# The output projection of the first pass as seven products too, and the sums of its weights made in that pass

## The chip, the cores and the metric

The kernel runs on one core of a Trainium2 chip. The metric is the time of one execution on the device, in microseconds (us). All data is float32.

## The reference, cut to what matters

Two transformer blocks work on 2048 tokens of width 512 (8 sequences of 256 tokens). The change lies in the attention of the first block, a linear attention with 32 heads of 128, whose result is projected back to width 512:

```
qkv  = silu(xn @ qkv_w.T)                  # 32 heads, q, k and v of 128 each
attn = (decay * (q @ k.T)) @ v             # per head and sequence, in causal form
gate = sigmoid(xn @ gate_w.T)
out  = (gate * norm_w * rms(attn)) @ out_w.T       # [tokens, 4096] @ [4096, 512]
```

A mixture of 16 experts (two for each token) and a shared expert are added to the same result; the second block (one more attention and 64 low-rank experts) comes last. The last product, with `out_w`, is the one that the change rewrites in a quarter of the tokens.

## The kernel before, in words

**Passes, units and products.** The attention runs in four passes (`i` from 0 to 3) over 512 tokens each, that is two sequences (`b`). A pass has eight units (`g`), each with four heads in two pairs. A unit computes q, k, v and gate for its heads in seven "outer" products, p1, p2, p6, p5, p3, p7, p4 (`ORDER`; `k` counts them from 0 to 6): it is a Strassen-like scheme in which seven products of sums of blocks stand for eight products of blocks. In passes 1 to 3 each outer product is again made of seven inner ones; in pass 0 the three of `RAW` (p1, p2, p4) are made of seven, and the other four in plain form (`Outer.plain`, eight inner products). One inner product is `product` (line 731), four matmuls into one PSUM bank.

**Weights in the first pass.** `weights` (lines 662 to 703) loads each outer product's weights from `in_w_att` into one of three ring buffers `w` (line 679), and blocks to be added into two staging buffers `st` (line 674). VectorE makes the outer sums; GpSimd makes four inner sums (`inner_sum`, line 692), and the last of them has the sums stored to DRAM in `ws` (line 694), from which the later passes load them ready made. A ring buffer is free for the load three outer products later when that store has landed. These steps are issued one per inner product, during the outer product before theirs. For the products of `RAW` the matmuls use GpSimd's inner sums already in the first pass.

**The output product.** When an outer product has completed a pair of heads for one sequence, a `Quarter` begins: activations, scores (lines 853 and 854), the product with v (865 and 866), a square for the norm (880, whose sum is made on GpSimd) and the gated result `gT`, [128, 2, 256] (885). `Unit.output` then queues the output product. In plain form (`project_plain`) each quarter gives two pieces of four matmuls, eight pieces in a unit. In the form of seven products (`project`, line 942) there are seven such pieces in a unit; four sums of `gT` are needed as operands. The weights of p1, p2 and p3 are quarters of `in_w_out` as they are; those of p4, p5, p6 and p7 are sums of quarters (p5's tile holds the fourth quarter until its sum is made in place). Before the change pass 0 is plain, pass 1 has seven products and makes the four sums of weights on GpSimd (`out_sum`, line 1002) and stores them in `wos` (line 1003), and passes 2 and 3 load them from there (line 987). The last unit of pass 3 is plain in both kernels.

**Accumulation.** Each piece is added on VectorE into `acc`, seven blocks of [128, 512] per pass (ScalarE copies the first ones). In the form of seven products the blocks are not yet the result: `combine` makes it out of them at the end of a pass with seven additions on GpSimd, and `finish` (line 642) follows.

**Order.** Pieces of a quarter, output products, sums of weights and the like are put on a list with a due time (`later`) and released by `slot()`, which runs once after each inner product, so that a unit has 49 slots; most pieces count, and a slot gives out one of them (two if more than 12 wait). ScalarE and GpSimd keep the order of the program. The order on TensorE, VectorE and SyncE, which issues nearly all DMAs, is made by a planner from the program's order and its own costs. Each engine, and SyncE's queue too, then works strictly in that order: an instruction that waits holds up what is behind it.

**Buffers.** There are seven tiles for output weights (`wo`, 256 KB each), five for `gT`, and three PSUM banks (`ps_sc`) for scores and output products.

The functions that the diff touches, and their callers:

Of the kernel before, what the change touches and what calls it, by code (L numbers as in the profile page):

```python
# [22 lines left out]
NCH = NT // CH  # L23
# [4 lines left out]
NG = H // HG  # L28
# [41 lines left out]
def block_kernel(  # L70
# [25 lines left out]
    nc = tc.nc  # L96
    mm = nc.tensor.matmul

    def tt(o, a, b, op, eng=None):
        (eng or nc.vector).tensor_tensor(o, a, b, op)  # L100
# [32 lines left out]
    def ps_sc():  # L133
        return ps.tile([P, 512], FP, tag="sc", name="ps_sc", bufs=3)
# [101 lines left out]
    def rsqrt(o, v, scale=1.0):  # L236

        nc.scalar.activation(o, v, AF.Sqrt, bias=eps_t, scale=scale)
        nc.vector.reciprocal(o, o)

    class Normal:


        def __init__(self, o, xc):
            self.o, self.xc = o, xc
            self.mv = small.tile([P, TPC, 2], FP, tag="mv", name="mv")
            self.rstd = small.tile([P, TPC], FP, tag="rstd", name="rstd")
# [144 lines left out]
    def add(o, a, b, eng=None):  # L392
        tt(o, a, b, ALU.add, eng)

    def sub(o, a, b, eng=None):
        tt(o, a, b, ALU.subtract, eng)
# [259 lines left out]
    with tc.tile_pool(name="attn", bufs=1) as attn, tc.manual_schedule(engines={mybir.EngineType.Activation, mybir.EngineType.Pool}):  # L656
# [90 lines left out]
        def later(after, f):  # L747
            pieces.append((now[0] + after, len(pieces), f))
            pieces.sort(key=lambda x: x[:2])
# [144 lines left out]
        class Unit:  # L894
            def __init__(self, i, g):
                self.i, self.g = i, g
                self.tiles = {}
                self.wo, self.decays = {}, []
                self.A, self.O = {}, {}
                self.plain = i == 0 or (i, g) == (NCH - 1, NG - 1)  # L900

# [4 lines left out]
            def output(self, b, pair, gT):  # L908

                if self.plain:  # L910
                    for t in range(2):
                        later(4 + t, partial(self.project_plain, b, pair, gT, t))
                    return
                A, O = self.A, self.O
                pool = nc.gpsimd
                A[b, pair] = gT
                if (b, pair) == (0, 0):
                    O["p1"] = gT
                    ready = (("p1", 4),)
                elif (b, pair) == (1, 0):  # L920
                    O["p7"] = self.gated()
                    sub(O["p7"], A[0, 0], gT, pool)
                    ready = (("p7", 6),)
                elif (b, pair) == (1, 1):
                    O["p4"] = gT
                    O["p5"], O["p6"] = A[1, 0], A[0, 0]
                    add(A[1, 0], A[1, 0], gT, pool)
                    sub(A[0, 0], A[1, 0], A[0, 0], pool)
                    ready = (("p4", 4), ("p5", 7), ("p6", 10))
                else:  # L930
                    O["p2"] = gT
                    O["p3"] = A[1, 1]
                    sub(A[1, 1], gT, O["p6"], pool)
                    ready = (("p2", 4), ("p3", 7))
                for p, after in ready:
                    later(after, partial(self.project, p))
# [40 lines left out]
            def load_out(self, k):  # L977

                if self.plain:
                    for h in range(2):  # L980
                        if k in (2, 4):
                            self.out_tile((k // 2 - 1, h), w_out[self.g, k // 2 - 1, h])
                    return
                at = dict(p1=(0, 0), p5=(0, 1), p2=(1, 0), p3=(1, 1))
                for p in {2: ("p1",), 3: ("p7", "p4", "p5"), 4: ("p6", "p2"), 5: ("p3",)}.get(k, ()):
                    if p in ("p4", "p5", "p6", "p7") and self.i > 1:
                        self.out_tile(p, wos[self.g][:, int(p[1]) - 4].rearrange("p (h n) -> p h n", h=2))
                    else:
                        self.out_tile(p, w_out[self.g, at[p][0], at[p][1]] if p in at else None)
                if k == 5 and self.i == 1:  # L990
                    for n in range(4):
                        later(6 + 2 * n, partial(self.out_sum, n))

            def out_tile(self, key, source):
                self.wo[key] = attn.tile([P, 2, C // 2], FP, tag="wo", name="wo", bufs=7)
# [28 lines left out]
            def done(self):  # L1024
                if self.g < NG - 1:
                    return
                i = self.i
                pr = ps_sc()

                def squares(ts):  # L1030
                    for t in ts:
                        for n in range(2):
                            mm(
                                pr[:, t : t + 1],
                                sums_[i][:, t // 2, n * S + t % 2 * P : n * S + (t % 2 + 1) * P], ones,
                                start=(n == 0), stop=(n == 1),
                            )

                def means():
                    squares((2, 3))  # L1040
                    rms = small.tile([P, TPC], FP, tag="rms", name="rms", bufs=NCH)
                    rsqrt(rms, pr[:, 0:TPC], 1.0 / (H * HD))
                    all_rms[i] = rms

                def store():
                    nc.sync.dma_start(out=xs_[i], in_=self.r)

                squares((0, 1))
                later(1, means)
                after = 2  # L1050
                if 0 < i < NCH - 1:
                    for n in range(7):
                        later(after + n, partial(combine, i, COMBINED[n : n + 1]))
                    after += 8
                if i + 1 < NCH:
                    for n in range(TPC):
                        later(after + 1 + n, partial(finish, i, self.r, (n,), tc.keep_in_program_order))
                    later(after + 1 + TPC, store)
# [251 lines left out]
        for n, (i, g, p) in enumerate(plan):  # L1310
# [5 lines left out]
            k = ORDER.index(p)  # L1316
# [494 lines left out]
```

## Time and profile before

| what | value |
|---|---|
| median of 3 runs | 2814.0 us (2809.46 to 2821.68) |
| the profiled execution: its own time | 2814.99 us |
| its span, first to last instruction | 2813.1 us |
| pass 0, about | 130 to 735 us of the span |
| passes 1, 2, 3, about | 735 to 1330, 1330 to 1925, 1925 to 2515 us |
| one unit of pass 0, about | 72 to 75 us |
| TensorE matmul busy, share of the span | 98% |
| TensorE weight load busy, share of the span | 90% |
| VectorE, ScalarE, GpSimd busy | 58%, 34%, 59% |
| DMA moved | 752.66 MB, 268 GB/s on average |

The span is what the profile divides up; 1.9 us lie around it. PE is TensorE's matmul row and PEld its weight loads, DVE VectorE, ACT ScalarE, POOL GpSimd, SPq SyncE's queue of DMA issues. A matmul in float32 stands in the trace as two instructions, so that a piece of four matmuls is "x8". L100 is a helper through which most element-wise operations go; its operations are told apart by the names of their tiles. "A <- B" in a list of waits means that A stood idle until B was done.

### The profile page before, as it was taken

How to read it: one execution, taken by the hardware profiler on the slowest of the kernel's cores; microseconds unless marked ns; L12 is line 12 of the kernel's file. 1: busy time of each engine (PE TensorE's matmuls, PEld its weight loads, DVE VectorE, ACT ScalarE, POOL GpSimd, SP SyncE). 2: the span in 40 equal slices, each digit the busy share in tenths (PEclk: the TensorE clock that was granted, in tenths of full speed). 3: DMA queues.
4: the chain of work that ended last, by engine and by line, in shares of the span. 5: the costliest groups of instructions: out<-in, count | busy, mean ns of one | idle time of the engine just before them, and what ended most of it. 6: DMA issues, size and time to landing. Idle time of an engine off the chain costs nothing.

```text
span 2813.1 us, 49529 instructions
## 1 busy us (share of the span) xinstructions
PE 2752.4 (98%) x19653; PEld 2538.8 (90%) x19653; DVE 1630.7 (58%) x2722; ACT 947.6 (34%) x1683; POOL 1645.8 (59%) x1414
## 2 busy tenths in 40 slices
PE   9999999998999999999999999999999999999999
PEld 5699999998989999999999999999999999987877
DVE  7666777776445555555545555555455555656663
ACT  4232222221433333333343333333433333432211
POOL 6467777775566676666755555556555567642220
PEclk9999999999999999999999999999999999999999
DMA  7888888887977877778877777787777788662211
GB/s 276 322 339 337 319 330 329 322 317 293 346 273 288 290 288 273 288 277 299 316 264 261 261 271 261 264 311 279 282 271 265 270 312 305 221 222 77 68 55 62
DMA packets 155062, 752.66 MB, mean 268 GB/s; under 512 B 18721, under 2 KB 25249, under 8 KB 103457
## 3 DMA queue, kind: packets, MB, share of 16 engines
q1 hardware_dynamic: 136672, 678.67, 64.7%
q0 software_dynamic: 17872, 70.32, 7.6%
q8 instruction: 155, 2.54, 0.3%
q14 instruction: 75, 0.61, 0.1%
q10 hardware_dynamic: 288, 0.52, 0.1%
HBM read 605.66 MB, written 142.99 MB: 266 GB/s over the span
## 4 chain that ended last, share of the span: by engine, by line
PE 85%; DVE 6%; DMA 4%; issue 2%; POOL 2%; ACT 1%; another core or an unknown queue 0%; SPq 0%; DVEq 0%; POOLq 0%; ACTq 0%
PE ps_a L731 25%; PE ps_e L731 12%; PE ps_sc L942 10%; PE ps_b L731 7%; PE ps_o L865 4%; PE ps_sc L962 3%; PE ps_sc L853 3%; PE ps_sc L800 3%; PE ps_a L1601 2%; PE ps_o L866 2%; PE ps_sc L854 2%; PE ps_a L1701 2%; DMA st<-in_w_att_dram 2%; DVE w L100 1%; PE ps_sc L812 1%
## 5 line engine op out<-in xcount | busy, mean ns | idle before, releaser
L731 PE MATMUL ps_a<-xt,w 128*128 128x128 f32 x5376 | 752.9, 276 | 17.2 <-DVE r L100 7.8
L731 PEld LDWEIGHTS ps_a<-xt,w 128*128 128x128 f32 x5376 | 687.8, 192 | 47.3 <-issue 14.1
L100 POOL TENSOR_TENSOR c<-c 128x512 f32<-128x512 f32 x240 | 305.5, 1288 | 268.9 <-DVE c L100 266.5
L1099 ACT COPY cp<-ps_a 128x512 f32<-128x512 f32 x384 | 224.3, 584 | 667.7 <-PE ps_a L731 642.3
L100 POOL TENSOR_TENSOR c<-c,r 128x512 f32<-128x512 f32 x264 | 346.3, 1334 | 166.7 <-DVE r L100 164.2
L731 PE MATMUL ps_e<-xt,w 128*128 128x128 f32 x2688 | 374.8, 276 | 5.2 <-DVE c L100 1.6
L100 POOL TENSOR_TENSOR w<-w 128x512 f32<-128x512 f32 x224 | 298.2, 1339 | 93.2 <-DVE w L100 44.7
L731 PEld LDWEIGHTS ps_e<-xt,w 128*128 128x128 f32 x2688 | 341.3, 192 | 12.1 <-issue 4.8
L731 PE MATMUL ps_a<-w,xt 128*128 128x128 f32 x1792 | 346.9, 275 | 0.0
L100 POOL TENSOR_TENSOR sums<-sums,sq 128x512 f32<-128x512 f32 x120 | 155.9, 1299 | 280.9 <-ACT sq L880 280.4
L942 PE MATMUL ps_sc<-wo,gT 128*128 128x256 f32 x1288 | 304.9, 380 | 2.4 <-POOL gT L100 2.4
L731 PEld LDWEIGHTS ps_a<-w,xt 128*128 128x128 f32 x1792 | 272.6, 192 | 0.0
L942 PEld LDWEIGHTS ps_sc<-wo,gT 128*128 128x128 f32 x1288 | 232.9, 190 | 30.5 <-issue 2.9
L100 DVE TENSOR_TENSOR acc<-ps_sc,acc 128x512 f32<-128x512 f32 x208 | 142.6, 689 | 192.6 <-PE ps_sc L942 151.1
L885 DVE SCALAR_TENSOR_TENSOR gT<-ps_o,nw,c 128x256 f32<-128x256 f32 x256 | 111.9, 478 | 214.9 <-ACT sq L880 205.9
L731 PE MATMUL ps_b<-xt,w 128*128 128x128 f32 x1536 | 216.0, 277 | 13.1 <-DVE w L100 6.2
L100 DVE TENSOR_TENSOR c<-ps_a,c 128x512 f32<-128x512 f32 x216 | 146.8, 687 | 123.3 <-PE ps_a L731 118.5
L731 PEld LDWEIGHTS ps_b<-xt,w 128*128 128x128 f32 x1536 | 196.1, 194 | 16.0 <-issue 12.6
L828 ACT ACTIVATE c<-c 128x512 f32<-128x512 f32 x256 | 150.4, 628 | 145.8 <-DVE c L100 127.0
L880 ACT ACTIVATE sq<-ps_o 128x512 f32<-128x512 f32 x120 | 71.7, 597 | 367.0 <-PE ps_o L866 359.5
L100 DVE TENSOR_TENSOR s<-ps_sc,decay 128x384 f32<-128x384 f32 x256 | 139.5, 553 | 81.5 <-PE ps_sc L854 76.8
L731 PE MATMUL ps_e<-w,xt 128*128 128x128 f32 x896 | 173.5, 275 | 0.0
(306 smaller groups left out, 4747.4 us busy)
## 6 DMA issues: line engine op xcount, KB each, us to landing
w<-in_w_att_dram SPq DMA_DIRECT2D x128, 1024.0 KB
st<-in_w_att_dram SPq DMA_DIRECT2D x32, 1024.0 KB
wo<-in_w_out_dram SPq DMA_DIRECT2D x113, 256.0 KB
decay<-dec SPq DMA_DIRECT2D x64, 384.0 KB
w<-ws0p SPq DMA_DIRECT2D x12, 1792.0 KB
w<-ws1p SPq DMA_DIRECT2D x12, 1792.0 KB
w<-ws2p SPq DMA_DIRECT2D x12, 1792.0 KB
w<-ws3p SPq DMA_DIRECT2D x12, 1792.0 KB
```

Source lines behind the costliest of these rows:

```text
L100: (eng or nc.vector).tensor_tensor(o, a, b, op)
L731: mm(bank[:, bass.ts(ty, P)], a, b, start=(first and ty == 0), stop=True, skip_group_check=True,)
L800: mm(pu[:, bass.ts(n, P)], w12[:, n, c, :], self.xeT[:, c, :], start=(c == 0), stop=(c == NC - 1),)
L828: nc.scalar.activation(qk, qk, AF.Silu)
L853: mm(p[:, 0:S], self.c[:, 2 * hh, P : 2 * P], q, start=True, stop=True)
L854: mm(p[:, S : S + P], self.c[:, 2 * hh + 1, P : 2 * P], q[:, 1, :], start=True, stop=True,)
L865: mm(po[:, bass.ts(hh, S)], v[:, 0, :], self.s[:, hh, 0:S], start=True, stop=False)
L880: nc.scalar.activation(sq, po, AF.Square)
L885: nc.vector.scalar_tensor_tensor(gT[:, h, :].rearrange("p (t n) -> p t n", t=2), po[:, bass.ts(h, S)].rearrange("p (t n) -> p t n", t=2), ...
L942: mm(py[:, bass.ts(t, S)], self.O[p][:, hh, bass.ts(t, P)], self.wo[p][:, hh, :], start=(t == 0 and hh == 0), stop=(hh == 1), skip_group_c ...
L962: mm(py[:, bass.ts(h, S)], gT[:, hh, bass.ts(t, P)], self.wo[pair, h][:, hh, :], start=(h == 0 and hh == 0), stop=(hh == 1), skip_group_ch ...
L1099: nc.scalar.copy(c, bank)
```

## The change

Pass 0 makes its output product in the form of seven products too, and makes and stores the sums of weights there. Pass 1 then loads all its output weights, as passes 2 and 3 do. Two of the four sums of `gT` are made on VectorE in pass 0. In pass 0 the tiles of a unit's output weights are all taken at k = 3 (four loads from `in_w_out` and three empty tiles) instead of two at k = 2 and two at k = 4, and the four sums of weights are due 8, 10, 12 and 14 slots after that. `combine` now follows pass 0 too, so that `finish` of pass 0 comes eight slots later.

```diff
@@ class Unit
-                self.plain = i == 0 or (i, g) == (NCH - 1, NG - 1)
+                self.plain = (i, g) == (NCH - 1, NG - 1)
@@ def output
                 pool = nc.gpsimd
+                soon = pool if self.i else nc.vector
                 A[b, pair] = gT
...
                     O["p7"] = self.gated()
-                    sub(O["p7"], A[0, 0], gT, pool)
+                    sub(O["p7"], A[0, 0], gT, soon)
                     ready = (("p7", 6),)
...
                     O["p3"] = A[1, 1]
-                    sub(A[1, 1], gT, O["p6"], pool)
+                    sub(A[1, 1], gT, O["p6"], soon)
                     ready = (("p2", 4), ("p3", 7))
@@ def load_out
-                for p in {2: ("p1",), 3: ("p7", "p4", "p5"), 4: ("p6", "p2"), 5: ("p3",)}.get(k, ()):
-                    if p in ("p4", "p5", "p6", "p7") and self.i > 1:
+                order = {2: ("p1",), 3: ("p7", "p4", "p5"), 4: ("p6", "p2"), 5: ("p3",)}
+                if self.i == 0:
+                    order = {3: ("p1", "p3", "p5", "p7", "p2", "p6", "p4")}
+                for p in order.get(k, ()):
+                    if p in ("p4", "p5", "p6", "p7") and self.i > 0:
                         self.out_tile(p, wos[self.g][:, int(p[1]) - 4].rearrange("p (h n) -> p h n", h=2))
                     else:
                         self.out_tile(p, w_out[self.g, at[p][0], at[p][1]] if p in at else None)
-                if k == 5 and self.i == 1:
+                if k == 3 and self.i == 0:
                     for n in range(4):
-                        later(6 + 2 * n, partial(self.out_sum, n))
+                        later(8 + 2 * n, partial(self.out_sum, n))
@@ def done
-                if 0 < i < NCH - 1:
+                if i < NCH - 1:
                     for n in range(7):
                         later(after + n, partial(combine, i, COMBINED[n : n + 1]))
                     after += 8
```

## The prediction

> **What bounds the kernel now.** I read the page's table of engines first, then the stretches by pass, then who waits for whom on TensorE in the first pass, then one unit of it in order of time. The table, and the four passes (time; busy us of PE, PEld, DVE, ACT and POOL, with instruction counts; granted clock; DMA share; GB/s):
>
> ```profile
> PE 2752.4 (98%) x19653; PEld 2538.8 (90%) x19653; DVE 1630.7 (58%) x2722; ACT 947.6 (34%) x1683; POOL 1645.8 (59%) x1414
> ...
> 130.00:735.00 605.00, 584.80 (x4451) 561.16 (x4451) 409.94 (x607) 160.94 (x279) 423.37 (x359) 0.99 0.86 326
> 735.00:1330.00 595.00, 589.72 (x4509) 559.64 (x4508) 314.49 (x480) 223.74 (x404) 389.12 (x314) 1.00 0.78 285
> 1330.00:1925.00 595.00, 588.50 (x4492) 560.38 (x4491) 317.39 (x473) 226.48 (x404) 343.13 (x277) 1.00 0.76 279
> ```
>
> TensorE is the bound in every pass: its weight loads fill 93 to 94% of each. The first pass is the tightest for the others: TensorE stands idle 605.0 - 584.8 = 20.2 us, against 5.3 and 6.5 in the next two, POOL is busy 70%, DVE 68%, and DMA 86%. So work taken from TensorE there is worth its full length only while POOL, DVE and DMA still deliver in time. Who holds TensorE up in six of the units (the engine that waits and whom for; us, times, longest), and what does it once, at 667 us:
>
> ```profile
> PE ps_b L731 <- issue: 3.8, 2, 2.0
> PE ps_a L731 <- POOL w L100: 3.5, 5, 1.3
> PE ps_b L731 <- DVE w L100: 6.2, 1, 6.2
> ```
>
> The 3.5 us are small, but they fall at one place in five units, the inner sums of p4's weights. One such place in POOL's and SyncE's order (start, length, what, and the idle time ahead):
>
> ```profile
> 528.74 1.27 POOL L100 TENSOR_TENSOR sums<-sums,sq 128x512 f32<-128x512 f32 x1
> 532.49 1.27 POOL L100 TENSOR_TENSOR w<-w 128x512 f32<-128x512 f32 x1 [2.48 <-DVE w L100]
> ...
> 535.20 4.02 POOL L100 TENSOR_TENSOR w<-w 128x512 f32<-128x512 f32 x3
> 542.75 5.21 POOL L100 TENSOR_TENSOR w<-w 128x512 f32<-128x512 f32 x4 [3.53 <-issue]
> ...
> 522.88 6.25 SPq L694 DMA_DIRECT2D ws5p<-w  x2
> 529.19 1.54 SPq L997 DMA_DIRECT2D wo<-in_w_out_dram  x2
> 534.88 4.36 SPq L679 DMA_DIRECT2D w<-in_w_att_dram  x2
> ```
>
> POOL has gaps of 2.48 and 3.53 us. The second ends when p4's weights have landed: their load went out at 534.88, after SyncE had waited 4.1 us for the store of p5's sums (issued 522.88), and TensorE waits 0.38 us for the third of these sums at 546.66. p4's chain, store, load, sums, product, has no slack. p2's has 3.2 us: its first sum is done at 561.7, its second product comes at 564.86.
>
> **What the Trainium skill says.** "Perfetto Trace Analysis", section Identifying the Most-Contended Engine: matmul busy time is a poor measure, weight-load time a good one; hence the 93% above, which agrees. "GPSIMD Engine Reference", section Key points: it shares its SBUF interfaces with VectorE, with contention against VectorE instructions with two SBUF inputs. The trace agrees: such additions into w take VectorE 0.63 us at 671.85, where POOL is idle, and 1.16 at 676.58, where POOL works beside. "DMA: Bandwidth & Descriptors", section Issuing engines are not separate DMA queues: all DMAs share 16 engines; so 8 MB more in the first pass lengthen the landing of what is already there. Between 525 and 540 us this trace shows a DMA share of 1.00 at 392 GB/s. "TensorE: Matmul & The Clock Gate", section What's actually happening: after an idle window of some 3.4 us the array runs at half clock for about as long. After the stall at 667 us the granted clock was 0.55 and 0.77 in the next slices of 5 us.
>
> **Part by part.**
>
> 1. *TensorE.* Eight pieces a unit become seven. A piece takes 1.73 us from its start to the next instruction (510.27 to 512.00). 8 units x 1.73 = **-13.8 us**, all on the bound. The piece goes from k = 0 and 1 of each unit: pieces in k = 2 to 5, the stretch of p4's chain, stay four.
>
> 2. *VectorE, first pass.* 60 additions and 4 copies into acc become 49 and 7 (ScalarE: 3 x 0.59 us more, idle 70%). DVE loses 11 x 0.69 = 7.6 us and gains 16 sums of gT. No row of before has these on DVE: bounds 0.63 and 1.26 us (the w sums just named; the row of w<-w on DVE means 1.259), I take 1.26: +20.2. Net +12.6 us over the pass, 1.6 a unit beside some 22 idle: nothing, covered by DVE's idle time in k = 0, 1 and 6. In k = 2 and 3 DVE is full (510 to 525), and the sum for p3 and two more additions, 2.6 us, fall there; p5's sums there stand 2.4 us ahead of POOL's need, p3's 3 us ahead of TensorE's. If that cover is short, up to 0.5 us a unit.
>
> 3. *POOL, first pass.* 16 sums of gT x 1.275 (row of gT<-gT) = 20.4, and 32 sums of weights x 1.50 (row of wo<-wo) = 48.0: 8.5 us a unit, busy from 56 to about 65 of 73. The sums of gT fall at k = 1, where POOL stood idle 8.38 us before 503.29: nothing. The sums of weights fall due at k = 4 and 5, three of them ahead of p7's inner sums and one among them: 4 x 1.5 = 6.0 us into gaps of 2.48 + 3.53 = 6.01. p4's sums then start when they did. But p7's end 6.0 - 2.5 = 3.5 us later, so does their store, and p2's load waits for that store: 3.5 us against a slack of 3.2, less the 1.73 that TensorE is now early. Bounds 0 and 2.0 us a unit; I take 0.3, since the wait before p2's load is for the landing, and not all of the shift need arrive there.
>
> 4. *DMA and SyncE, first pass.* 32 stores of 256 KB = 8.4 MB more, 1.05 MB a unit. Output weights: as many loads, all at k = 3; 0.5 MB leave the full stretch at 529 and 0.5 MB leave 500, and 1 MB comes at 514, beside a trough (share 0.22 from 510 to 515). p3's tile is used until slot 23 of the next unit and its load is due at slot 21, so SyncE can stand some 3 us; p7's block and weights are queued behind, and p5's store behind those. SyncE waited there for p6's store until 522.46 anyway. For p4's chain: at best 0.5 MB less ahead of it, -1.2 us a unit (at 392 GB/s; only the present 0.4 to 1.3 can be gained); at worst 1.05 MB more, +2.7, and 0.8 of standing, +3.5. I take +0.1, since both signs are open. SyncE's waits for the sums before their stores (102 us for 32 in the second pass) move here; p1's load stands behind the last.
>
> 5. *Second pass.* 48 us of POOL work and its waits leave, 32 loads replace 32 stores. The third pass is of that form already, and TensorE idles 6.5 us in it against 5.3. Nothing; bounds -2 and +2. Its output loads wait for tiles 234 us in the third pass against 78 without TensorE standing, so that too is covered, by weights loaded a product ahead.
>
> 6. *Between the passes.* Seven combines x 1.3 = 9.1 us of POOL, finish eight slots later; a staging buffer is held as long, and the first copy into the next acc waits. The start of the third pass shows just that: ScalarE waits 9.2 us for finish, TensorE idles 1.2 and 1.7 us in two slices, no more than at the start of the second now (3.6 us). Nothing; bounds -1 and +3, a late expert's load the risk.
>
> Sum: -13.8 + 8 x (0.3 + 0.1) = -10.6, about **-11 us**. The profiled execution has 2815.0, the median 2814.0: so 2804 against the one, **2803** against the other.
>
> **Rivals.**
>
> *The stalls go too.* If early loads into the trough and fewer stores between p5's sums and p4's load give p4's chain slack, the 3.5 us of waits there go, and the one stall of 6.2 us at 667 with its slow clock after it (some 2 us), which comes from a staging block that landed late. For: the stretch 525 to 540 is full and loses loads. Against: it gains three stores. -13.8 - 3.5 - 6.2 - 2 = -25: **2789**.
>
> *p4's chain takes over (slower).* It has no slack, and TensorE's saving lies elsewhere, so each us by which p5's store or p4's load is late is a us of the unit. It decides from 1.73 us a unit, where the saving is gone; at 3.5 (item 4) the result is 8 x 3.5 - 13.8 = +14; with 1 us of half clock after each stall, +22: **2836**. For: DMA share 1.00 there, POOL's gaps filled to the last 0.1 us. Against: the trough at 510, and the planner, which may put stores behind the load.
>
> *The saving is eaten half.* Stalls of 0.8 to 1.7 us a unit, by the same places and p2's: -7 to 0, **2810**.
>
> That the change does not do what it says I see no way for: all eight units of the pass get the seven products.
>
> **How the numbers follow.** Forecast 0.50 (own range 2796 to 2808), stalls go too 0.17, half eaten 0.12, p4's chain 0.21. A measurement of this kernel can tell 0.5%, 14 us, from no change: 2800 and 2828. The forecast lies across the first border: its waits may be nil and the third item's 0.3 with it, and of its 0.50 I put 0.25 below 2800. Faster 0.25 + 0.17 = 0.42; same 0.25 + 0.12 = 0.37; slower 0.21. Range 2787 to 2832, from the first rival's value to most of the second's.
>
> **What would show it.** Right: 56 pieces at line 942 in the first pass and that pass 10 to 14 us shorter, the others as long; waits of p4's product for POOL at no more than 1.5 us a unit; sums of weights 1.5 us each inside POOL's two gaps; p4's load 12 us after p5's store as now. Wrong: waits of TensorE for POOL's or DVE's w above 14 us in the first pass; p5's store or p4's load later than now by over 1.7 us against the unit's start; a first pass as long as before; or a second pass that changes by over 3 us.

## The result, and the profile after

The kernel after takes **2857.75 us** (median of 4 runs, 2854.18 to 2860.86) against 2815.3 us for the kernel before beside it: a ratio of 1.015, 95% interval 1.0123 to 1.0177. The forecast was 2803 us, with a range that ended at 2832. The change makes the kernel 1.5% slower.

The profiled execution took 2854.18 us, with a span of 2852.5. The line of its page that answers to the first one of before:

```profile
PE 2753.9 (97%) x19589; PEld 2530.1 (89%) x19589; DVE 1643.0 (58%) x2727; ACT 947.5 (33%) x1686; POOL 1676.6 (59%) x1437
```

TensorE has less to do and is busy as long. The same stretches as before, cut at the new ends of the passes (time; busy us and counts of PE, PEld, DVE, ACT, POOL; granted clock; DMA share; GB/s):

```profile
130.00:774.00 644.00, 583.77 (x4373) 548.55 (x4373) 407.59 (x606) 162.56 (x282) 490.50 (x405) 0.99 0.83 316
774.00:1360.00 586.00, 580.07 (x4419) 550.43 (x4419) 315.72 (x469) 214.79 (x389) 347.02 (x285) 1.00 0.80 286
1360.00:1960.00 600.00, 594.85 (x4547) 566.44 (x4546) 322.58 (x482) 230.63 (x412) 344.30 (x279) 1.00 0.77 276
```

The loss lies in the first pass: 644 us in place of 605 in these stretches, which are cut by hand. From the first decay load of one pass to that of the next, the same mark in both kernels, the first pass is 43.0 us longer (632.9 against 589.9), the second 4.2 us shorter (604.4 against 608.6) and the third 3.2 us longer. In the first stretch TensorE stands idle for 644.00 - 583.77 = 60.2 us in place of 20.2. In the later ones the idle time is 5.9 and 5.2 us, against 5.3 and 6.5 before. The 39 us are made up as follows: -13.8 for the pieces that are gone, +40.0 of idle time, and the rest, 12.8, is busy time with the same work. Of the 12.8 us, 2.8 are a lower granted clock (8.5 us lost to it in the pass, 5.7 before). By an estimate, some 7 more are the ends of matmuls ahead of waits: TensorE has 62 idle gaps in this pass in place of 20, and its busy row shows about 0.16 us more at each. The rest stays unexplained. A unit of the pass (from one unit's first decay load to the next one's, mean of the second to the seventh) takes 78.6 us in place of 73.3.

Who holds TensorE up in the first pass (us, times, longest):

```profile
PE ps_a L731 <- DVE w L100: 18.7, 11, 13.3
PE ps_b L731 <- DVE w L100: 12.5, 6, 2.2
PE ps_a L731 <- POOL w L100: 9.9, 9, 1.4
PE ps_o L865 <- DVE s L100: 4.8, 8, 0.6
```

VectorE's outer sums, which held it up once before, for 6.2 us, now do so in every unit but the first. The second row is one place, 1.6 to 2.2 us in each of six units: p5's second product. To see what makes it late, I followed the chain of waits inside one unit, which begins at 504.79 us. Each row is a start, a length, and what the end of the unit depended on at that moment ("issue" is time for which the trace names nothing):

```profile
523.82 1.74 PE ps_sc L943 x8
525.56 2.81 issue
528.37 0.54 POOL w L100
...
530.53 1.26 POOL c L100
531.79 1.23 POOL w L100
533.03 1.24 POOL c L100
...
534.29 0.69 DVE c L100
...
537.41 3.43 DVE w L100 x2
540.84 0.04 issue
540.88 2.54 PE ps_b L731 x16
```

For 15.3 us, from 525.56 to 540.88, the unit does not depend on TensorE. It waits for VectorE and GpSimd in turn: GpSimd's inner sums of p6, which follow VectorE's outer ones, the addition of p2's results to c on GpSimd, VectorE's own additions to c behind these, p5's outer sums. A second detour of the same unit runs from 558.8 to 573.9, to p4's inner sums, with one sum of weights in it. In the unit of before from 482.72 the chain is TensorE's for 67.3 of 72.6 us (48 to 69 in the others from the second to the seventh), with 5.2 us at p4's sums. In the kernel after it is TensorE's for 48.0 us in the unit shown, 31 to 34 in four others and 56 in one.

In four of these six units, though not in the one shown, the second detour runs through p5's store and p4's load, the chain that the prediction feared. In the unit from 426.11:

```profile
471.61 11.47 DMA ws4p<-w
483.13 8.60 DMA w<-in_w_att_dram
```

Against the unit's start the store is at 45.5 us and the load at 57.0; in the unit of before that the prediction shows they are at 40.2 and 52.2. Both are some 5 us later, but 11.5 us lie between them as against 12.0 before: this chain began later, as p5's sums did (below), and the transfers hardly lengthened it.

The head of the detour is the order on VectorE. Its instructions in that unit of the kernel after (start, length, what, idle time ahead):

```profile
517.59 0.69 DVE L100 TENSOR_TENSOR c<-ps_e,cp 128x512 f32<-128x512 f32 x1 [4.57 <-PE ps_e L731]
...
521.68 0.69 DVE L100 TENSOR_TENSOR c<-ps_a,c 128x512 f32<-128x512 f32 x1 [1.25 <-PE ps_a L731]
522.55 0.69 DVE L100 TENSOR_TENSOR acc<-ps_sc,acc 128x512 f32<-128x512 f32 x1 [0.18 <-PE ps_sc L943]
523.16 2.49 DVE L100 TENSOR_TENSOR w<-w,st 128x512 f32<-128x512 f32 x4
525.56 0.87 DVE L885 SCALAR_TENSOR_TENSOR gT<-ps_o,nw,c 128x256 f32<-128x256 f32 x2
526.35 2.49 DVE L100 TENSOR_TENSOR w<-w,st 128x512 f32<-128x512 f32 x4
...
534.29 0.69 DVE L100 TENSOR_TENSOR c<-ps_e,c 128x512 f32<-128x512 f32 x1 [1.77 <-POOL c L100]
...
536.09 5.34 DVE L100 TENSOR_TENSOR w<-w,st 128x512 f32<-128x512 f32 x4
```

And in the kernel before, where the unit begins at 482.72:

```profile
495.70 1.28 DVE L100 TENSOR_TENSOR w<-w,st 128x512 f32<-128x512 f32 x2
497.85 0.69 DVE L100 TENSOR_TENSOR acc<-ps_sc,acc 128x512 f32<-128x512 f32 x1 [0.86 <-PE ps_sc L962]
...
500.12 2.49 DVE L100 TENSOR_TENSOR w<-w,st 128x512 f32<-128x512 f32 x4
502.53 0.68 DVE L100 TENSOR_TENSOR c<-ps_e,cp 128x512 f32<-128x512 f32 x1
...
509.36 5.09 DVE L100 TENSOR_TENSOR w<-w,st 128x512 f32<-128x512 f32 x4
```

The first w<-w,st are p6's eight sums, the last four are p5's. Before, p6's sums stand ahead of p2's additions (c<-ps_e,cp and so on) and start 13.0 us after the unit's start. After, the planner has put p2's additions, down to that of its own last result (c<-ps_a,c at 521.68), and an addition to acc ahead of them. These wait for TensorE (4.57, 1.25 and 0.18 us in the lines shown), and p6's sums start at 18.4 us. So p5's, which follow, start at 31.3 us in place of 26.6, and p5's second product at 36.1 in place of 33.4.

One more reading agrees that TensorE alone no longer sets a unit's length. Two units in succession, with the granted clock in the third column from the end:

```profile
426.11:504.79 78.68, 72.44 (x545) 67.80 (x545) 52.98 (x76) 19.55 (x35) 64.65 (x55) 1.00 0.83 318
504.79:583.26 78.47, 73.85 (x549) 69.33 (x548) 50.80 (x76) 19.79 (x35) 63.87 (x55) 0.98 0.84 319
```

In the second one TensorE ran at half clock for 3.4 us after the wait at 540.88, which takes 1.7 us of work away. It is no longer than the first: the time that TensorE loses there it waits less elsewhere. That is one pair of units; the experiments have to show it.

### The profile page after: what moved, and what is told of

Its sections match the earlier page's. It is cut to its first block, busy times and chain, and to the rows that moved or that the text cites. A ratio compares the mean times of both kernels' runs of the same rounds, so it can differ in the third digit from the quotient of the medians.

```text
span 2852.5 us, 49486 instructions
## 1 busy us (share of the span) xinstructions
PE 2753.9 (97%) x19589; PEld 2530.1 (89%) x19589; DVE 1643.0 (58%) x2727; ACT 947.5 (33%) x1686; POOL 1676.6 (59%) x1437
## 4 chain that ended last, share of the span: by engine, by line
PE 79%; DVE 7%; DMA 7%; issue 3%; POOL 3%; ACT 0%; SPq 0%; DVEq 0%; POOLq 0%; ACTq 0%
PE ps_a L731 23%; PE ps_sc L943 12%; PE ps_e L731 11%; PE ps_b L731 6%; PE ps_o L865 3%; PE ps_sc L853 3%; PE ps_sc L800 3%; DMA w<-in_w_att_dram 3%; DVE w L100 2%; POOL w L100 2%; PE ps_o L866 2%; PE ps_sc L854 2%; PE ps_a L1705 2%; PE ps_sc L812 1%; PE ps_a L1605 1%
## 5 line engine op out<-in xcount | busy, mean ns | idle before, releaser
L731 PE MATMUL ps_a<-xt,w 128*128 128x128 f32 x5376 | 758.9, 277 | 50.9 <-DVE w L100 18.7
L943 PE MATMUL ps_sc<-wo,gT 128*128 128x256 f32 x1736 | 416.7, 381 | 5.9 <-DVE gT L885 3.3
L100 POOL TENSOR_TENSOR w<-w 128x512 f32<-128x512 f32 x224 | 307.2, 1379 | 117.3 <-issue 52.0
L943 PEld LDWEIGHTS ps_sc<-wo,gT 128*128 128x128 f32 x1736 | 312.4, 191 | 44.7 <-DVE gT L885 5.7
L100 DVE TENSOR_TENSOR acc<-ps_sc,acc 128x512 f32<-128x512 f32 x197 | 136.0, 690 | 182.5 <-PE ps_sc L943 172.0
L731 PE MATMUL ps_b<-xt,w 128*128 128x128 f32 x1536 | 216.5, 277 | 14.0 <-DVE w L100 12.5
L731 PEld LDWEIGHTS ps_b<-xt,w 128*128 128x128 f32 x1536 | 195.9, 194 | 17.2 <-DVE w L100 13.6
```

Of the source, the lines that this page charges most:

```text
L731: mm(bank[:, bass.ts(ty, P)], a, b, start=(first and ty == 0), stop=True, skip_group_check=True,)
L943: mm(py[:, bass.ts(t, S)], self.O[p][:, hh, bass.ts(t, P)], self.wo[p][:, hh, :], start=(t == 0 and hh == 0), stop=(hh == 1), skip_group_c ...
```

## The experiments

Two theories stood at the start. **Order, or "late sums"**: the order on VectorE makes p6's and p5's sums late. **"Load", later "more work" or "stores"**: what was added on GpSimd, in the transfers and in SyncE's queue costs the time. Where a kernel leaves something out, its expectation says what. Each time is a median beside the kernel before on the same chip (2813.7 to 2815.3 us); one execution of sums_no_stores, at 8441 us, is left out of its median. "unit" is the mean length of the second to the seventh unit of the first pass, from the profile.

| run | us | ratio to before, 95% interval | unit |
|---|---|---|---|
| before | 2815 | | 73.3 |
| after | 2857.8 | 1.0150 (1.0123 to 1.0177) | 78.6 |
| seven_only | 2828.4 | 1.0055 (1.0033 to 1.0076) | 73.9 |
| sums_only | 2900.0 | 1.0305 (1.0282 to 1.0329) | 84.5 |
| order_back | 2859.0 | 1.0159 (1.0138 to 1.0181) | 79.1 |
| gt_on_pool | 2898.8 | 1.0304 (1.0282 to 1.0326) | 84.1 |
| before_sums_late | 2840.8 | 1.0100 (1.0076 to 1.0124) | 76.7 |
| seven_sums_first | 2832.2 | 1.0066 (1.0044 to 1.0087) | 75.2 |
| stores_no_sums | 2859.7 | 1.0166 (1.0141 to 1.0190) | 79.4 |
| sums_on_vector | 2857.6 | 1.0152 (1.0130 to 1.0174) | 79.1 |
| after_order_seven | 2838.7 | 1.0086 (1.0069 to 1.0102) | 76.1 |
| after_first_shared | 2838.0 | 1.0073 (1.0051 to 1.0094) | 76.4 |
| seven_shared | 2828.9 | 1.0050 (1.0034 to 1.0067) | 75.8 |
| before_shared | 2841.1 | 1.0099 (1.0082 to 1.0116) | 78.2 |
| sums_no_stores | 2831.2 | 1.0061 (1.0041 to 1.0081) | 74.3 |
| after_order_five | 2836.7 | 1.0075 (1.0058 to 1.0092) | 75.6 |
| before_table_later | 2817.2 | 1.0009 (1.0000 to 1.0018) | 73.3 |
| best_of_all | 2822.8 | 1.0032 (1.0022 to 1.0042) | 73.6 |
| order_seven_no_five | 2845.5 | 1.0118 (1.0101 to 1.0135) | 77.4 |
| no_stores_no_five | 2847.7 | 1.0123 (1.0106 to 1.0140) | 78.1 |

### The two halves of the change

**seven_only**

```diff
-                    order = {3: ("p1", "p3", "p5", "p7", "p2", "p6", "p4")}
+                    order = {3: ("p1", "p3", "p5", "p2")}
...
+                    self.wo["p7"], self.wo["p6"], self.wo["p4"] = (self.wo[p] for p in ("p5", "p3", "p2"))
```

> Seven products in the first pass, but no sums of weights made there: p4, p6 and p7 multiply by the tiles of p2, p3 and p5 as they are (their products are not the reference's), and the second pass makes and stores the sums as before. Theory 'order on VectorE' (the planner now puts p6's outer sums behind the adds of p2's results, and the chain VectorE - GpSimd - VectorE then holds up p5's weights): the order is only partly back here (one add ahead of the sums instead of five), so most of the 4.4 us a unit should go; 2805 to 2830. Rival 'load' (GpSimd's sums of weights and the stores fill the first pass): with both gone the saved piece shows in full, 2798 to 2806, and TensorE waits no longer for p5's outer sums.

**sums_only** (before, and in pass 0)

```diff
+                    if k == 4 and self.i == 0:
...
+                        for n in range(4):
+                            later(1 + 2 * n, partial(self.out_sum, n))
```

> The first pass stays plain, but the sums of weights are made and stored there (four loads at k = 2 and 4 as before, sums due one, three, five and seven slots after k = 4), and the second pass loads them. The sum for p4 reuses p7's tile once that is stored. Theory 'load': most of the loss is here, 2840 to 2870. Theory 'order on VectorE': the planner's order is half changed here (four of eight outer sums behind one add of p2's results), 2812 to 2830.

The products alone, which take the work away, already make the kernel 13 us slower. They should have brought it to 2801, so 27 us are lost with the products, and 29 more with the sums and stores. sums_only fell outside both ranges and tells nothing of the sums' price, because I put them where their loads are under way. GpSimd, in its fixed order, stood still for them (its waits in that kernel; us, times, longest):

```profile
POOL wo L100 <- DMA wo<-in_w_out_dram: 69.1, 7, 12.7
```

That is ten us in a unit, and the unit is 11 us longer than before.

### Order, and GpSimd's load

**order_back** pins p2's additions behind what stands before them in the program, p6's sums among it.

```diff
-                        add(o, bank, c)
+                        kept = tc.keep_in_program_order if (u.i, p) == (0, "p2") else lambda ins: ins
+                        kept(nc.vector.tensor_tensor(o, bank, c, ALU.add))
```

> The changed kernel, with the adds of p2's results in the first pass kept behind p6's outer sums on VectorE, as they stood in the kernel before. Theory 'order on VectorE': the two waits of 0.57 and 2.18 us for p5's outer sums in each of seven units and the half clock after them (1.7 us) go: some 4 us a unit, 2820 to 2832. Rival 'load': the sums wait for their landing instead, 2850 to 2865.

**gt_on_pool**

```diff
-                soon = pool if self.i else nc.vector
+                soon = pool
```

> The changed kernel, with all four sums of gT on GpSimd also in the first pass. The order of p6's outer sums against p2's adds stays as in the changed kernel. If VectorE's own load were the cause (two sums of 0.7 us a unit), the waits for p5's outer sums shrink by about as much: 2845 to 2852. Under 'order on VectorE' nothing changes: 2850 to 2862; under 'load' GpSimd has 2.6 us more a unit and it gets slower: 2860 to 2885.

Taken alone the two pointed to the load: no gain from the order, and 41 us from 2.6 us more on GpSimd in a unit. The traces say otherwise. In gt_on_pool TensorE now waits for these sums themselves:

```profile
PE ps_sc L943 <- POOL gT L100: 51.3, 15, 4.9
```

They stand behind p6's and p2's work in GpSimd's order, with a product due: it is their place that costs, more than their 2.6 us. And order_back had not put the order back. The planner had moved two additions to acc ahead of p6's sums in place of p2's, which waited 4.9 and 2.8 us for TensorE, and the sums began 17.2 us after the unit's start in place of 18.4. It could not decide.

**before_sums_late** asks the converse: p6's sums behind p2's additions in the kernel before, with nothing added.

```diff
-                        add(o, bank, c)
+                        previous["added"] = nc.vector.tensor_tensor(o, bank, c, ALU.add)
...
-                cur.following = outers[n + 1]
+                cur.following = None if p == "p2" else outers[n + 1]
...
             cur.p2()
             cur.p5()
+            if (i, p) == (0, "p2"):
+                cur.following = outers[n + 1]
+                with tc.issue_after(previous["added"].ins):
+                    for _ in range(6):
+                        cur.following.step()
```

> The kernel before, with one change of order: on VectorE the eight outer sums of p6 (w<-w,st) stand behind the additions of p2's results, where the kernel after has them, in place of ahead of them. No work is added or removed. Theory 'late sums' (p6's outer sums start 18 us after a unit's start in place of 13.5, so the store, the staging buffer and p5's sums behind them are late by as much, in every one of the eight units): 2835 to 2860 us. Rival 'more work' (what was added on GpSimd and in transfers costs the time, and the order on VectorE only shows it): 2812 to 2820 us.

`previous["added"]` is p2's last such addition.

**seven_sums_first** holds the additions to acc, p2's additions and the operations that make one quarter's gT behind p6's last sum in seven_only (`tc.issue_after` around them), and issues the sums earlier.

> As seven_only (seven products in the first pass, no sums of weights made there; the products p7, p6 and p4 take other weights, so the output is not the reference's), with p6's outer sums pinned ahead of p2's additions on VectorE, the order of the kernel before. 'Late sums': 2800 to 2810 us, so the saving of 14 us comes back, or most of it. 'More work' (the sums of gT on VectorE and GpSimd): 2824 to 2832 us, as seven_only.

Such an order alone costs the kernel before 26 us, and TensorE's wait is at the same kind of row (before_sums_late, first pass):

```profile
PE ps_a L731 <- DVE w L100: 20.6, 8, 10.5
```

So a late p6 alone can cost tens of us. The 26 us are not the price of the change's own order, though: p6's sums start 20.8 to 26.5 us into the unit there, later than the 18.4 of the kernel after. Nor does seven_sums_first bear out the simple form of the theory: with p6's first sum at 12.7 us the kernel isn't faster. But it hardly tests it. p6's last sum came no earlier than in seven_only (20.8 us against 20.7), and p5's sums came later still (31.3 us against 27.4), since the additions that had been put off now stood ahead of them.

### Sums or stores

**stores_no_sums** and **sums_on_vector**

```diff
-                sub(w[p], w[a], w[b], nc.gpsimd)
+                if self.i:                                  # stores_no_sums
+                    sub(w[p], w[a], w[b], nc.gpsimd)
...
+                sub(w[p], w[a], w[b], nc.vector)            # sums_on_vector
```

> The kernel after without the 32 sums of weights on GpSimd: the four stores of a unit go out as before, with loaded tiles in place of sums (the output is not the reference's), and three of the seven tiles are the same ones as others. VectorE's order is that of the kernel after. 'GpSimd's time' (4 x 1.27 us a unit in its order is what sets the unit): 2826 to 2834 us, as seven_only. 'Stores' (8.4 MB more in SyncE's queue and the transfers): 2850 to 2862 us. 'Late sums' alone, with VectorE's order kept: 2848 to 2860 us too, and then p5's outer sums are the wait that is left, 2 us a unit.

> The kernel after with the 32 sums of weights on VectorE in place of GpSimd, stores and loads unchanged; the whole computation. 'GpSimd's time': 2826 to 2838 us. 'Stores' or 'late sums': 2850 to 2865 us. If VectorE's own 4 x 0.7 us a unit come into the way of p5's sums, above 2865 us.

**sums_no_stores**

```diff
                 sub(w[p], w[a], w[b], nc.gpsimd)
+                if self.i == 0:
+                    return
                 nc.sync.dma_start(
```

with pass 1 making and storing them as in the kernel before.

> The kernel after, where the first pass makes its sums of weights for its own products but doesn't store them; the second pass makes and stores them as in the kernel before. The whole computation; 4 x 1.27 us a unit of GpSimd stay in the first pass. Without the stores VectorE's planned order is that of seven_only (p6's sums ahead of p3's addition to c). 'Order' theory and 'stores' theory: 2826 to 2836 us, as seven_only. If the sums on GpSimd cost by themselves: 2842 us or more.

Without the sums on GpSimd the kernel is as slow as after (2859.7, 2857.6); with the stores moved to the second pass it is back near seven_only (2831.2). So GpSimd's 42 us of sums cost nothing that shows, and the stores bring 25 us more in the first pass than in the second. But the stores also change the order: in stores_no_sums and in sums_on_vector VectorE has the order of the kernel after, and in sums_no_stores that of seven_only. Its lines in the unit of sums_no_stores from 486.88 us:

```profile
503.15 2.49 DVE L100 TENSOR_TENSOR w<-w,st 128x512 f32<-128x512 f32 x4
505.55 0.68 DVE L100 TENSOR_TENSOR acc<-ps_sc,acc 128x512 f32<-128x512 f32 x1
506.15 2.49 DVE L100 TENSOR_TENSOR w<-w,st 128x512 f32<-128x512 f32 x4
508.56 0.68 DVE L100 TENSOR_TENSOR c<-ps_a,c 128x512 f32<-128x512 f32 x1
```

The addition of p2's last result (c<-ps_a,c) and one to acc, which the kernel after has ahead of p6's sums, stand behind them or among them.

**after_order_seven** therefore keeps stores, loads and sums and changes VectorE's order alone: the addition to acc, the addition of p2's last result and the two operations that make gT go behind p6's sums.

```diff
+        def behind_sums():
+            last = previous.get("hold")
+            return tc.issue_after(last.ins) if last else nullcontext()
...
-                    add(o, py, o)
+                    with behind_sums():
+                        add(o, py, o)
...
+            if p == "p5":
+                previous["hold"] = None
...
+            if (i, p) == (0, "p2"):
+                previous["hold"] = previous["last"]
```

> The kernel after with one change of order on VectorE: p6's outer sums stand ahead of an acc addition and of p3's addition to c, where seven_only has them; loads, stores and all sums as in the kernel after. 'Late sums' (what parts the kernel after from seven_only is that these two instructions wait for TensorE ahead of the sums): 2828 to 2840 us. 'Stores' (the 4 stores of a unit and their place in SyncE's queue): 2853 to 2862 us.

It gains 19 us of the 25. p6's eight sums run without a break from 511.82, 15.5 us after the unit's start:

```profile
509.06 0.69 DVE L100 TENSOR_TENSOR c<-ps_e,cp 128x512 f32<-128x512 f32 x1 [4.57 <-PE ps_e L738]
...
511.82 5.65 DVE L694 TENSOR_TENSOR w<-w,st 128x512 f32<-128x512 f32 x8
```

The wait of 4.57 us ahead of p2's additions is still there, without the loss. What counted were the instructions behind it, which waited again ahead of p6's sums. The first detour of the chain shrinks from 15.3 us to 4.2:

```profile
523.27 1.74 PE ps_sc L951 x8
...
525.64 3.55 DVE w L694 x3
529.20 0.04 issue
529.24 1.83 PE ps_b L738 x14
```

So most of what the stores cost, they cost by the order that the planner made with them in the program. The remaining 6 us or so may be the stores themselves or what is left of the order: p5's sums start 29.1 to 29.7 us into the unit here, 27.2 to 27.7 in sums_no_stores and some 31 in the kernel after. That isn't settled; the intervals of after_order_seven and sums_no_stores overlap.

### What is left with the products

**after_first_shared, seven_shared, before_shared**: p5 adds the block that p6 has loaded, and waits for no staging buffer and no transfer of its own. In the first, p6's sums also stand first.

```diff
+                if p == "p5":
+                    outer = [(add, previous["s3"])]
+                elif p == "p6":
+                    zero = block(0)
+                    previous["s3"] = block(3)
+                    outer = [(add, previous["s3"]), (sub, zero)]
```

> The kernel after with p6's outer sums ahead of p2's additions on VectorE (the order of the kernel before), and with p5 taking the block of weights that p6 has already loaded into the staging buffer in place of loading it again: p5's sums then wait for no free staging buffer and no transfer of their own, and a unit loads one block of 1 MB less. 'Late sums': 2795 to 2812 us, below the kernel before, with no wait of TensorE for p5's sums left. 'Stores' or 'GpSimd': 2835 to 2858 us.

> As seven_only (seven products in the first pass, no sums of weights made there; the products p7, p6 and p4 take other weights, so the output is not the reference's), with p5 using p6's loaded block as in after_first_shared. 'Late sums' (p5's sums are late because their block is loaded late): 2793 to 2806 us. If what costs seven_only 27 us more than its products save lies elsewhere: 2820 to 2832 us.

> The kernel before with p5 using p6's loaded block; nothing else changed. 'Late sums' says that p5's sums are just in time there (1 to 2 us of waiting a unit at most) and TensorE is the bound: 2800 to 2815 us. If the chain of loads and sums bounded the kernel before as well, below 2795 us.

None made its kernel faster: against the runs without the edit the first is as fast as after_order_seven and the second as seven_only, inside the ranges that their rivals had. The kernel before lost 26 us with a load less in each unit, outside both ranges. In it the planner placed p6's sums early among p1's and p2's additions. The blocks hadn't landed there, VectorE stood for up to 7.9 us with these additions queued behind, and TensorE waited 26.9 us for additions to c. Both ways are wrong: sums behind additions that wait for TensorE, and additions behind sums that wait for a transfer.

**after_order_five** puts p5's sums ahead of p6's last addition as well; **before_table_later** and **best_of_all** move one slow transfer of the last unit (`later(4, read_table)` to `later(24, ...)`). best_of_all is sums_no_stores with both orders of sums and the later table.

> after_order_seven with one more change of order on VectorE: p5's four outer sums stand ahead of p6's last addition and of the acc addition behind it. 'Order' theory: the wait of 1.5 us a unit for p5's sums shrinks by about 1 us, and the slower matmuls after it go: 2822 to 2834 us. Rival 'another wait takes its place' (p4's sums on GpSimd, s, p7's sums): 2835 to 2842 us, as after_order_seven.

> The kernel before with the read of the table put off by 20 slots in the last unit of the first pass, behind p7's block, so that p5's block and its sums don't wait behind this slow transfer. The wait of 6.2 us in that unit goes, or most of it: 2806 to 2812 us. Rival: the read now holds the staging buffer from another block and as much is waited there: 2812 to 2820 us.

> sums_no_stores with p6's and p5's outer sums first on VectorE (as in after_order_five) and with the read of the table put off (as in before_table_later). The whole computation. 'Order' theory with the last unit's wait gone (12 us): 2803 to 2818 us, so about the kernel before. If what is left of the loss has another cause (p4's load, GpSimd): 2819 to 2832 us.

after_order_five gains nothing that shows over after_order_seven. p5's sums begin 2.0 to 2.6 us earlier but end only 0.2 to 0.7 us earlier: they now run beside GpSimd and take 6.2 us in place of 4.1. Moving the table moves the wait: what VectorE's sums waited for (6.2 us of TensorE before, 13.3 after), p1's load now waits for. The two rows, from before_table_later and best_of_all:

```profile
PE ps_a L731 <- DMA w<-in_w_att_dram: 10.8, 1, 10.8
```

```profile
PE ps_a L740 <- DMA w<-in_w_att_dram: 13.0, 1, 13.0
PE ps_b L740 <- issue: 12.7, 7, 2.1
```

best_of_all is the fastest version with seven products that computes everything, 35 us better than after and still 0.3% slower than before. Its units are almost as long as those of before, with 1.7 us less of products in each: one wait of 1.7 to 2.1 us is left in each of six units (the second row). The trace calls it "issue", but where it falls says more. It is at p7's second product, 52 us into the unit, and in all six units that product starts 0.10 us after VectorE's third outer sum of p7 has ended. The lines of one unit, which begins at 336.29:

```profile
384.54 4.48 DVE L694 TENSOR_TENSOR w<-w,st 128x512 f32<-128x512 f32 x4 [0.64 <-DMA st<-in_w_att_dram]
388.52 0.91 PE L740 MATMUL ps_b<-xt,w 128*128 128x128 f32 x6 [1.77 <-issue]
```

VectorE waits 0.5 to 1.1 us there for p7's block. The block's load is issued 39 to 42 us into the unit, 31 to 34 in the kernel before. So with p5's sums early enough, p7's are the next to be late.

**order_seven_no_five, no_stores_no_five** leave out p5's sums and their load (`p5=[(add, 3)]` deleted) to see whether this chain is the whole rest.

> after_order_seven without p5's outer sums: the four additions on VectorE and the load of their block are left out in the first pass, so p5 takes its raw weights and the output is not the reference's. If the chain that ends in p5's sums (p6's block, p6's sums, the free staging buffer, p5's block, p5's sums) is what holds the unit at 75 to 76 us: 2812 to 2828 us, with no wait left at p5's second product. If another wait takes its place (p4's sums on GpSimd, the stores): 2832 to 2842 us.

> sums_no_stores without p5's outer sums and the load of their block (the output is not the reference's), with p6's outer sums held behind p2's additions, about where sums_no_stores has them. If p5's chain is what is left of the loss there: 2798 to 2815 us, so the products' saving of 14 us comes through or nearly. If not: 2824 to 2834 us.

They are 7 and 16 us slower than with the sums (the second also holds p6's sums behind p2's additions). With p5's block gone, the staging buffers and the order fall out differently, and other waits take the place. In order_seven_no_five (first pass):

```profile
PE ps_a L738 <- issue: 14.8, 6, 3.1
PE ps_b L738 <- DMA w<-in_w_att_dram: 9.8, 1, 9.8
```

The "issue" waits in these two kernels too end 0.10 us after an outer sum of p7, whose block lands late: VectorE waits 1.3 to 8 us for it. So p5's chain is not the one thing that holds the rest; p7's is as close behind.

## Why the prediction was wrong

- **Item 1, TensorE, right and of no use.** The pieces are gone: 432 matmul rows of the output product in the first pass in place of 496, which is eight pieces of eight. Their 13.8 us did not reach the end. The prediction's premise, "TensorE is the bound in every pass", rested on weight-load time of 93%. That says how full the engine is, not that nothing stands as close behind it. In the first pass loops of loads and sums of about a unit's length did, as the chain shows (48 to 69 of some 73 us on TensorE even before). seven_only, without the sums and the stores, shows where the saving went: in its middle units TensorE waits 1.55 us a unit for p5's third and fourth outer sums; p5's sums start 27.3 us into the unit there, no earlier than the 26.6 of before.
- **Item 2, VectorE: the step that failed.** The durations were put high (a sum of gT on VectorE took 1.03 us in the mean, 0.68 for p3's and up to 1.77 for p7's, against 1.26) and the conclusion "covered by DVE's idle time in k = 0, 1 and 6" was wrong all the same. It took each instruction to stay in its place. The order on VectorE is made anew when the program changes, and p6's sums went from 13.0 to 18.4 us, behind p2's additions and one to acc, which wait for TensorE. The cover I had read for p5's sums, "2.4 us ahead of POOL's need", was then gone: they started 4.7 us later. This is the term that was allowed "up to 0.5 us a unit". VectorE's order alone gave 19 us back (after_order_seven), 2.4 us for each of eight units, and an order still later cost 26 us without any of the change (before_sums_late).
- **Item 3, POOL: right for the sums of weights, by its size and by runs.** They took 1.32 us in the mean against 1.50 assumed, and taking them away altogether, with the stores kept, changes nothing measurable. For the sums of gT that stayed on GpSimd nothing was tested; moving the other two there costs 41 us, through their place in the queue.
- **Item 4, DMA and SyncE: mis-sized, for a reason that it didn't have.** I weighed megabytes and places in SyncE's queue and took +0.1 us a unit. The stores bring 25 us, and at least most of that through VectorE's order. TensorE's waits for GpSimd's sums grew from 3.5 to 9.9 us, 0.8 us a unit: p4's chain did get later, but it isn't the main wait.
- **Items 5 and 6, right on idle time**: the later passes idle as before, within 1.3 us. Between decay loads the second pass got 4.2 us shorter, more than the bounds of item 5 and than the 3 us that the prediction named as a sign of error; no run looked into that.
- **The rivals.** "p4's chain takes over" had the sign and named the kind of event, a chain without slack that loses more than TensorE gains. But it put the chain at p4 and its price in transfers, and its 2836 is 22 us short. p5's store and p4's load did come later than the 1.7 us that were named as a sign of error, by some 5 us, but with 11.5 to 12.5 us between them as against 12.0. The other sign, "waits of TensorE for POOL's or DVE's w above 14 us", reads 18.7 + 12.5 + 9.9 = 41 us, of which 13.3 are the one wait of the last unit.
- **The one-off.** The wait of the last unit for p5's block, behind the table's slow read, went from 6.2 to 13.3 us; no step of mine had it.

What stays open. seven_only stands 27 us above eight units with 1.73 us less, best_of_all some 22. The unit lengths in seven_only divide its 27 us into about 14 in the six middle units, 7 in the last and 3 in the first, and its trace puts some 9 of the 14 at the waits for p5's sums named above. best_of_all agrees: with p5's sums earlier, that wait is gone, and one for p7's sums has come in its place. But this is read from traces. No run took all the waits away at once, among them those for s of 0.6 us a unit, and what lengthens the first and the last unit was not tested.

## What to carry to other kernels

Before counting a saving on the busiest engine, follow the chain of waits through one period of the loop: where it leaves that engine for long stretches, the loop may have a second bound, and the saving may end there. The length of these stretches is no price: in best_of_all the chain is on TensorE for 61 to 71 of 73.6 us, and the saving is still lost. When a planner orders an engine, an edit elsewhere is also an edit of that order. Compare the orders of the two programs on each engine, above all for in-order engines on which sums of fresh loads mix with additions of fresh results, before pricing the instructions; and when an experiment on order shows nothing, look first whether the order is really what was meant.

## What the runs showed of the hardware

- After a wait of 2.18 us TensorE ran at half clock (0.50) from 542.3 to 545.7 us, in one unit and not in the one before it, with the same wait. In the kernel before it did so from 653.5 to 656.8 us, after a wait of 2.03 us. The page "TensorE: Matmul & The Clock Gate" of the Trainium skill, section What's actually happening, speaks of an idle window of some 3.4 us; the trace shows less than that in one piece.
- VectorE's additions into w took 0.62 us each where GpSimd stood (523.16, four in 2.49) and 1.34 beside it (536.09, four in 5.34), so a block of sums can double in length when GpSimd works beside it. In the kernels before and after every such sum beside which GpSimd stood still takes 0.67 to 0.69 us from its start to its own end; beside GpSimd some still do, and some take up to 1.76.
